# Order of loads, weight preparation and routing at the joints of layer 0 in a four-layer macaron model

## The chip, the cores and the metric

The kernel runs on one core of a Trainium2 chip. A core has a matrix engine (TensorE, PE in the profile; PEld is its weight load), a vector engine (DVE), a scalar engine (ACT) that also evaluates functions from tables, GpSimd (POOL), and SyncE (SP), which here only issues DMA transfers. Each engine works through its own instructions in order and waits on semaphores. SP and ACT each have a DMA queue of their own, so a DMA that ACT issues stands among ACT's other instructions. The metric is the device time of one execution in microseconds (us), lower is better, shown as a median over several runs.

## What is computed

x has 8 sequences of 256 tokens with 128 features, 2048 tokens in all. Four layers follow one another, each a "macaron": half a feed-forward network (FFN), attention or a mixer, and the same FFN again.

```python
x = x + 0.5 * _L0_ffn_ref(_layernorm(x, axis=-1), ...)
x = x + _L0_attn_ref(_layernorm(x, axis=-1), ...)
x = x + 0.5 * _L0_ffn_ref(_layernorm(x, axis=-1), ...)
x = x + 0.5 * _L1_ffn_ref(_layernorm(x, axis=-1), ...)
x = x + _L1_attn_ref(_layernorm(x, axis=-1), ...)
...
```

Layer 0's FFN has 16 experts. Each expert picks its own 256 tokens by the largest scores, and a shared expert treats all tokens. Layer 0's attention has 16 causal heads with rotary positions. Layer 1's FFN has 8 experts of which each token uses two, computed densely with weights that are zero for the others; layer 1's mixer is a selective scan. Layer 2's FFN uses binarized weights, which are computed from `w1` and `w2` alone. The parts that the change touches:

```python
# layer 0 FFN
scores = jax.nn.softmax(flat_x @ gate_w.T, axis=-1).T
topk_weight, topk_idx = jax.lax.top_k(scores, C)        # C = 256 tokens per expert
xg = flat_x[topk_idx]
eo = einsum('eci,edi->ecd', gelu(xg Wg) * (xg Wu), Wd) * topk_weight[..., None]
out = zeros.at[topk_idx].add(eo) + shared
# layer 1 FFN
probs = softmax(xf @ router_w.T) * mask_of_top2
probs = probs / (probs.sum(-1, keepdims=True) + 1e-09)
h = silu(xf gate_w + gate_b) * (xf up_w + up_b)
y = einsum('ne,ned->nd', probs, h down_w + down_b)
# layer 2 FFN, for w1 and w2
alpha = mean(abs(w), axis=1, keepdims=True); bw = alpha * sign(w)
```

## The kernel before

x stays on the core as 16 tiles of 128 tokens by 128 features (`x_res`). Layer 0 treats all 16 tiles at once: FFN (stage 0), attention (stage 1), FFN (stage 2). From layer 1 on the tokens are cut into two halves, a and b, of 4 sequences (class `Half`), whose stages are put into the order listed in `run`: (a,3), then a's scan beside b's first FFN of layer 1, then b's scan beside a's second FFN, and so on. `beside_experts` interleaves the two: the FFN is a generator that yields between its units.

Nobody writes the final order of instructions. A scheduler takes the program's order as priorities and lists the instructions of each engine as their inputs are expected to be ready. An order that must hold can be imposed with a dependency that carries no wait (`add_manual_dep` with class NoSync): it only places an instruction behind another one. DMA transfers of SP and ACT share eight semaphores in turn, so a ninth transfer is issued only when the one before it on its semaphore has landed.

The steps that the change and the prediction touch, with the line numbers of the profile:

- Layer 0's expert weights are 12 transfers of 1 MB (three tensors, four experts in each), issued at L278 at the head of each layer-0 FFN, two of three from SP and one of three from ACT. The norm's bn_stats and bn_aggr (L238, L239) give mean and variance, `rstd` (L226 to L229) the root on ACT, L242 the normalized `xn`, L222 its transposes and L212/L214 their copies to `xnT`. Router: lg (L330), maximum and subtraction (L332, L334), exp (L335), then a bisection for each expert's threshold from L349 on. The shared expert (L431 to L436) runs beside it.
- Expert results are scattered into two accumulators in DRAM; L501 reads them back in eight transfers of 256 KB, from SP and ACT in turn, and L503 adds each into `x_res`. Only four `back` tiles exist.
- Layer 0's attention starts with a norm, then rotations (L727 to L730) and splits into parts (L554 to L557, `sp_r`), which L581 and L582 bring into the layout for scores.
- `l2_weights` (L775 to L794) loads layer 2's `w1` and `w2` (256 KB each) and binarizes and transposes them. It is called after layer 0.
- Layer 1's FFN (`l1_ffn`, L905 on): norm, router lg (L918), maximum L922, exp L925, the choice of two by DVE operations on 128x64 elements (L926 to L951), then the share of the down bias (transposes `prps` L957, products `pb` L963, added at L965), then 8 experts of 2 units of 512 tokens: pg and pu (L976, L978) twice, gs on ACT (L980), hT on DVE (L981), eight po (L987), ys on ACT (L993), x += ys (L995). Expert weights (`w_e`, 384 KB each, three buffers) are loaded at L900, by SP and ACT in turn. The PSUM tiles of pg, pu, lg, prps and the transposes share three buffers; po and pb share a single one.
- Layer 1's scan (`l1_attn`) starts at L1018 and ends with `pout` (L1137).

## Time and profile before

| What | us |
|---|---|
| median of 3 runs (2953.71 to 2966.58) | 2960.93 |
| the profiled execution | 2962.04 |
| its span, first to last instruction | 2960.2 |
| PE busy in the span | 2434.9 (82%) |
| DVE busy | 1592.9 (54%) |
| ACT busy | 1038.1 (35%) |
| POOL busy | 319.2 (11%) |

The mean granted TensorE clock is 0.861 of full speed. The stages that matter here lie at these places of the span: first layer-0 FFN 0 to about 226, attention 226 to 501, second layer-0 FFN 501 to about 728, first layer-1 FFN to 867, then the scans beside the other half's FFN.

In a timeline of the profile each row has the start, the duration, the engine, the line, the operation, output and inputs, shapes and count; in brackets stands how long the engine was idle before and what ended that. "ACTq" and "SPq" are DMA issues by those engines. Rows of windows give busy time (and instruction count) of PE, PEld, DVE, ACT and POOL in a stretch of time, then the granted clock, the DMA engines' busy share and GB/s. All times count from the start of the span.

### The profile page before, as it was taken

What the parts mean: (1) busy time and instruction counts of PE and PEld (TensorE: products, weight loads), DVE (VectorE), ACT (ScalarE), POOL (GpSimd) and SP (SyncE); (2) the same over time, 40 slices, a digit from 0 to 9 for tenths busy, and PEclk for the clock granted to TensorE, in tenths of its full rate; (3) what the DMA queues carried; (4) which work ended last, traced back from release to release, by engine and by line L of the source; (5) the groups of instructions that cost most, each with busy time, mean ns of one, the idle gap of its engine ahead of it and who ended that gap; (6) DMA issues with size and microseconds to landing.
All of it is one profiled execution on the core that took longest, in us unless ns stands there. A gap on an engine that the chain in (4) does not pass through costs nothing.

```text
span 2960.2 us, 40483 instructions
## 1 busy us (share of the span) xinstructions
PE 2434.9 (82%) x16194; PEld 1636.4 (55%) x16194; DVE 1592.9 (54%) x3704; ACT 1038.1 (35%) x1760; POOL 319.2 (11%) x441
## 2 busy tenths in 40 slices
PE   5784888585898889778887699789789789869999
PEld 3572555374554445465456557556556456545666
DVE  6535443834458888658464753554552644453332
ACT  1021333111358576325461332431234422223322
POOL 0371110064000000000000000000300100110000
PEclk9695798688799989867985699899989879979999
DMA  7134333223000000120012000100030100120100
GB/s 247 20 41 110 84 98 146 71 37 78 27 20 26 22 11 16 30 86 23 16 45 75 2 15 22 48 1 23 25 89 5 60 1 15 33 69 22 41 22 22
DMA packets 103018, 136.56 MB, mean 46 GB/s; under 512 B 15161, under 2 KB 84094, under 8 KB 96702
## 3 DMA queue, kind: packets, MB, share of 16 engines
q1 hardware_dynamic: 62858, 84.66, 9.2%
q10 hardware_dynamic: 27684, 39.61, 4.1%
q0 software_dynamic: 12288, 9.71, 2.4%
q8 instruction: 127, 2.08, 0.3%
q14 instruction: 61, 0.50, 0.1%
HBM read 106.27 MB, written 27.53 MB: 45 GB/s over the span
## 4 chain that ended last, share of the span: by engine, by line
PE 50%; DVE 15%; ACT 5%; issue 2%; POOL 1%; DMA 1%; ACTq 0%; DVEq 0%; POOLq 0%; SPq 0%
PE po L1556 7%; PE ph L1544 7%; PE po L987 3%; PE fl L1263 3%; PE pu L978 2%; PE pg L976 2%; PE pbc L1690 2%; PE ctx L649 2%; PE sc L1696 2%; PE y L1710 1%; PE tp L222 1%; DVE h L1116 1%; PE po L1160 1%; DVE hT L981 1%; PE y L1128 1%
## 5 line engine op out<-in xcount | busy, mean ns | idle before, releaser
L1556 PEld LDWEIGHTS po<-w_e,hT 128*128 128x128 f32 x2048 | 259.2, 194 | 71.5 <-issue 45.6
L1556 PE MATMUL po<-w_e,hT 128*128 128x128 f32 x2048 | 277.2, 280 | 10.5 <-DVE hT L1550 8.9
L1544 PE MATMUL ph<-x2T,w_e 128*128 128x512 f32 x512 | 266.5, 626 | 3.2 <-ACT hT L1552 2.8
L1552 ACT ACTIVATE hT<-ph,w_l_cols 128x512 f32<-128x512 f32 x192 | 131.1, 686 | 303.7 <-PE ph L1544 298.1
L602 DVE TENSOR_REDUCE nm<-sc 128x3 f32<-128x384 f32 (+1 forms) x192 | 130.6, 689 | 131.1 <-PE sc L600 130.0
L987 PEld LDWEIGHTS po<-w_e,hT 128*128 128x128 f32 x1024 | 138.3, 202 | 92.5 <-DVE hT L981 52.7
L987 PE MATMUL po<-w_e,hT 128*128 128x128 f32 x1024 | 151.2, 292 | 26.2 <-DVE hT L981 25.5
L639 ACT ACTIVATE pr_e<-scT 128x384 f32<-128x384 f32 (+1 forms) x192 | 111.7, 597 | 168.6 <-PE scT L636 160.7
L222 PE MATMUL tp<-c_ident,xn 128*128 128x128 f32 x208 | 59.0, 405 | 126.9 <-DVE xn L242 112.5
L1562 DVE SCALAR_TENSOR_TENSOR x_res<-po,gt,x_res 128x128 f32<-128x128 f32 x256 | 78.1, 358 | 127.5 <-PE po L1556 127.3
L978 PE MATMUL pu<-xnT,w_e 128*128 128x512 f32 x256 | 135.5, 611 | 10.0 <-ACT gs L980 10.0
L981 DVE SCALAR_TENSOR_TENSOR hT<-pu,w_l_bias,gs 128x512 f32<-128x512 f32 x128 | 95.0, 745 | 86.0 <-PE pu L978 85.3
L976 PE MATMUL pg<-xnT,w_e 128*128 128x512 f32 x256 | 136.8, 616 | 0.0
L481 ACT ACTIVATE gs<-pg 128x512 f32<-128x512 f32 x64 | 38.2, 597 | 252.1 <-PE pg L476 252.1
L980 ACT ACTIVATE gs<-pg,w_l_bias 128x512 f32<-128x512 f32 x128 | 87.7, 689 | 104.8 <-PE pg L976 101.2
L1544 PEld LDWEIGHTS ph<-x2T,w_e 128*128 128x128 f32 x512 | 85.2, 196 | 68.4 <-issue 33.1
L222 PEld LDWEIGHTS tp<-c_ident,xn 128*128 128x128 f32 x208 | 35.3, 177 | 148.6 <-DVE xn L242 72.7
L649 PE MATMUL ctx<-pr_e,vz 128*32 128x256 f32 x512 | 109.2, 402 | 2.8 <-ACT pr_e L639 2.7
L494 POOL DMA_INDIRECT l_acc<-eo,idx x64 | 101.9, 1592 | 34.9 <-DVE eo L493 15.1
L598 PE MATMUL sc<-ks,qs 72*128 72x256 bf16 x256 | 78.2, 306 | 27.5 <-DMA ks<-l_parts 17.5
L1702 DVE TENSOR_TENSOR gw<-sc,dec 128x768 f32<-128x768 f32 x64 | 61.2, 956 | 73.0 <-PE sc L1696 72.8
L993 ACT ACTIVATE ys<-po,pr 128x128 f32<-128x128 f32 x256 | 73.3, 368 | 71.4 <-PE po L987 71.2
(603 smaller groups left out, 5182.1 us busy)
## 6 DMA issues: line engine op xcount, KB each, us to landing
l_parts<-sT SPq DMA_DIRECT2D x48, 192.0 KB, 2.1
qs<-l_parts SPq DMA_DIRECT2D x16, 576.0 KB
w_l_wu<-in_l_wu ACTq DMA_DIRECT2D x8, 1024.0 KB, 8.9
w_l_wg<-in_l_wg SPq DMA_DIRECT2D x8, 1024.0 KB, 14.5
w_l_wd<-in_l_wd SPq DMA_DIRECT2D x8, 1024.0 KB
w_e<-in_l_e SPq DMA_DIRECT2D x16, 512.0 KB, 3.3
w_e<-in_l_e ACTq DMA_DIRECT2D x16, 512.0 KB, 3.6
w_e<-in_l_e ACTq DMA_DIRECT2D x16, 384.0 KB, 4.0
```

The source lines that it names most:

```text
L222: self.nc.tensor.transpose(ps[:, i * P : (i + 1) * P], src_of(g + i), self.ident)
L494: nc.gpsimd.indirect_dma_start(out=accs[h][:, :], out_offset=bass.IndirectOffsetOnAxis(ap=idx[:, j : j + 1], axis=0), in_=eo[:, h, :], in_ ...
L602: nc.vector.tensor_reduce(blocks[:, hp * pr : hp * pr + hp, :], sc[:, :, 0:384].rearrange("p h (k t) -> p h k t", t=P), AX.X, ALU.max, neg ...
L639: nc.scalar.activation(pe, sc[:, :, 0:384], AF.Exp, scale=float(1.0 / np.sqrt(np.float32(8.0))))
L649: nc.tensor.matmul(o, z, pe[:, 0:S], start=(j == 0), stop=False)
L976: self.keep_pace(nc.tensor.matmul(pg, wg[:, c], xnT[:, cols], start=True, stop=True), part)
L978: self.keep_pace(nc.tensor.matmul(pu, wu[:, c], xnT[:, cols], start=True, stop=True), part)
L981: nc.vector.scalar_tensor_tensor(hT[:, k, :], pu, w["l1_bias"][:, 1, e, k : k + 1], gs, ALU.add, ALU.mult)
L987: nc.tensor.matmul(po[:, i, :], hT[:, k, i * P : (i + 1) * P], wd[:, k * P : (k + 1) * P], start=(k == 0), stop=(k == 1),)
L1544: mm = nc.tensor.matmul(ps, we[:, k * P : (k + 1) * P], xnew[:, 512 * g : 512 * g + 512], start=True, stop=True)
L1552: nc.scalar.activation(hT[:, k, :], ps, AF.Relu, bias=bias)
L1556: nc.tensor.matmul(po[:, i, :], hT[:, k, i * P : (i + 1) * P], we[:, (4 + k) * P : (5 + k) * P], start=(k == 0), stop=(k == 3),)
```

## The change

Five things are changed; no operation is added or removed.

1. The loads of layer 0's experts become a function of their own. In the first FFN all 12 are issued by ACT and are ordered behind the root of the norm; the second FFN issues them as before.
2. Layer 1's expert loads are ordered behind the last read-backs of the same queue (`backs`).
3. `l2_weights` is called between the attention and the second layer-0 FFN. Its temporary tiles lie on the other side of the memory, and its PSUM pool has one buffer instead of two.
4. Where a scan runs beside the other half's FFN, that FFN's first bn_stats is ordered behind the first half's finished routing, and its first transpose behind the first half's fourth unit of experts (`hold`, `held`).
5. In layer 1's FFN the part of the down bias becomes `biases()`, called ahead of the third expert, with its transposes ordered behind the pg of the unit before.

```diff
         self.flip = 0
+        self.backs = [None, None]
...
         pass
+
+    def held(self, inst, queue):
+        pass
+
+    def behind(self, inst, mark):
+
+        dep = mybir.DependencyInfo(mybir.DependencyClass.NoSync, mybir.DependencyReason.DATA)
+        self.tc.add_manual_dep(inst.ins, mark.ins.name, dep, reason="what is needed first goes first")
...
             for i in range(m):
-                self.nc.tensor.transpose(ps[:, i * P : (i + 1) * P], src_of(g + i), self.ident)
+                self.held(self.nc.tensor.transpose(ps[:, i * P : (i + 1) * P], src_of(g + i), self.ident), "tensor")
             self.evict(dst[:, g * P : (g + m) * P], ps[:, : m * P])
...
         self.nc.vector.tensor_scalar(s, var, eps, None, ALU.add)
-        self.nc.scalar.activation(s, s, AF.Sqrt)
+        self.root = self.nc.scalar.activation(s, s, AF.Sqrt)
         self.nc.vector.reciprocal(s, s)
...
         for t in range(NT):
-            nc.vector.bn_stats(st[:, t, :], self.x[:, t, :])
+            self.held(nc.vector.bn_stats(st[:, t, :], self.x[:, t, :]), "vector")
             nc.vector.bn_aggr(mv[:, t, :], st[:, t, :])
...
             w[n] = pool.tile(list(src.shape), F32, name=f"w_{n}", tag=f"w_{n}")
+        return w
+
+    def l0_experts_in(self, w, after=None):
+
         for e in range(0, 16, 4):
-            for i, n in enumerate(w):
-                (self.nc.sync, self.nc.scalar)[i % 2].dma_start(w[n][:, e : e + 4], self.ins[n][:, e : e + 4])
-        return w
+            for i, n in enumerate(("l0_wg", "l0_wu", "l0_wd")):
+                eng = self.nc.scalar if after else (self.nc.sync, self.nc.scalar)[i % 2]
+                dma = eng.dma_start(w[n][:, e : e + 4], self.ins[n][:, e : e + 4])
+                if after:
+                    self.behind(dma, after)
...
-    def l0_ffn(self, w):
+    def l0_ffn(self, w, first):
         nc, tc = self.nc, self.tc
...
             w = w | self.l0_experts(ctx.enter_context(tc.tile_pool(name="l0x", bufs=1, side="right", reuse_waits="tile")))
+            if not first:
+                self.l0_experts_in(w)
             pool = ctx.enter_context(tc.tile_pool(name="l0f", bufs=1, reuse_waits="tile"))
...
                 xn, xnT = self.norm(rp, psA, width=W)
+                if first:
+                    self.l0_experts_in(w, self.root)
                 lg = ps1.tile([P, NT, 16], F32, name="lg", tag="pre")
...
                         back = ep.tile([P, 4, D], F32, name="back", tag="back", bufs=4)
-                        (nc.sync, nc.scalar)[k].dma_start(back, accv[k][:, 4 * g : 4 * g + 4, :])
+                        self.backs[k] = (nc.sync, nc.scalar)[k].dma_start(back, accv[k][:, 4 * g : 4 * g + 4, :])
                         xs = self.x[:, 4 * g : 4 * g + 4, :].rearrange("p t d -> p (t d)")
...
         with ExitStack() as ctx:
-            tmp = ctx.enter_context(tc.tile_pool(name="l2b", bufs=1, reuse_waits="tile"))
-            psum = ctx.enter_context(tc.tile_pool(name="l2bps", bufs=2, space=PSUM, reuse_waits="tile"))
+            tmp = ctx.enter_context(tc.tile_pool(name="l2b", bufs=1, side="right", reuse_waits="tile"))
+            psum = ctx.enter_context(tc.tile_pool(name="l2bps", bufs=1, space=PSUM, reuse_waits="tile"))
             w1, w2 = self.load(tmp, "l2_w1"), self.load(tmp, "l2_w2")
...
         tc = self.tc
-        with tc.tile_pool(name="l0w", bufs=1, side="right", reuse_waits="tile") as wp:
-            w0 = self.l0_weights(wp) if (on(0) or on(1) or on(2)) else None
-            if on(0):
-                self.l0_ffn(w0)
-            if on(1):
-                self.l0_attn(wp)
-            if on(2):
-                self.l0_ffn(w0)
-
-
-
         with tc.tile_pool(name="l2w", bufs=1, reuse_waits="tile") as late:
-            w2 = self.l2_weights(late) if (on(6) or on(8)) else None
+            with tc.tile_pool(name="l0w", bufs=1, side="right", reuse_waits="tile") as wp:
+                w0 = self.l0_weights(wp) if (on(0) or on(1) or on(2)) else None
+                if on(0):
+                    self.l0_ffn(w0, True)
+                if on(1):
+                    self.l0_attn(wp)
+
+                w2 = self.l2_weights(late) if (on(6) or on(8)) else None
+                if on(2):
+                    self.l0_ffn(w0, False)
+
+
+
             a, b = (Half(self, k, w2) for k in range(2))
...
         self.steps, self.pace, self.marks = [], [], None
+        self.backs, self.units, self.hold = chip.backs, [], {}
...
+    def held(self, inst, queue):
+
+        mark = self.hold.pop(queue, None)
+        if mark is not None:
+            self.behind(inst, mark)
+
     def beside_experts(self, other):
...
         other.pace, other.marks = self.steps, self.SCAN_MARKS
+        if self.units:
+            other.hold = {"vector": self.routed, "tensor": self.units[3]}
         fill = other.l1_ffn()
...
             t = pool.tile([P, src.shape[2]], F32, name="w_e", tag="w_e", bufs=3)
-            (self.nc.sync, self.nc.scalar)[e % 2].dma_start(t, src[e])
+            dma = (self.nc.sync, self.nc.scalar)[e % 2].dma_start(t, src[e])
+            if self.backs[e % 2] is not None:
+                self.behind(dma, self.backs[e % 2])
             yield e, t
...
             nc.vector.tensor_scalar(sm, sm, 0.5, None, ALU.mult)
-            nc.vector.tensor_tensor(pr, pr, wide(sm), ALU.mult)
-            prT = pool.tile([E, T], F32, name="prT", tag="prT")
-            G = T // 512
-            for g in range(G):
-                ps = psum.tile([E, 512], F32, name="prps", tag="h")
-                for i in range(4):
-                    nc.tensor.transpose(ps[:, i * P : (i + 1) * P], pr[:, 4 * g + i, :], self.ident)
-                self.evict(prT[:, 512 * g : 512 * g + 512], ps)
-            for g in range(G):
-                po = pso.tile([P, 4, D], F32, name="pb", tag="o")
-                for i in range(4):
-                    t = 4 * g + i
-                    nc.tensor.matmul(po[:, i, :], prT[:, t * P : (t + 1) * P], w["l1_bd"], start=True, stop=True)
-                xs = self.x[:, 4 * g : 4 * g + 4, :]
-                nc.vector.tensor_tensor(xs, xs, po, ALU.add)
+            self.routed = nc.vector.tensor_tensor(pr, pr, wide(sm), ALU.mult)
+
+            def biases():
+                prT = pool.tile([E, T], F32, name="prT", tag="prT")
+                for g in range(G):
+                    ps = psum.tile([E, 512], F32, name="prps", tag="h")
+                    for i in range(4):
+                        tr = nc.tensor.transpose(ps[:, i * P : (i + 1) * P], pr[:, 4 * g + i, :], self.ident)
+                        self.behind(tr, self.units[-1])
+                    self.evict(prT[:, 512 * g : 512 * g + 512], ps)
+                for g in range(G):
+                    po = pso.tile([P, 4, D], F32, name="pb", tag="o")
+                    for i in range(4):
+                        t = 4 * g + i
+                        nc.tensor.matmul(po[:, i, :], prT[:, t * P : (t + 1) * P], w["l1_bd"], start=True, stop=True)
+                    xs = self.x[:, 4 * g : 4 * g + 4, :]
+                    nc.vector.tensor_tensor(xs, xs, po, ALU.add)
+
+            G, self.units = T // 512, []
             for e, we in self.experts(pool, "l1_e"):
...
                     part = (G * e + g) / (8 * G)
+                    if (e, g) == (2, 0):
+                        biases()
                     yield part
...
                         pg = psum.tile([P, 512], F32, name="pg", tag="h")
-                        self.keep_pace(nc.tensor.matmul(pg, wg[:, c], xnT[:, cols], start=True, stop=True), part)
+                        mm = nc.tensor.matmul(pg, wg[:, c], xnT[:, cols], start=True, stop=True)
+                        self.keep_pace(mm, part)
                         pu = psum.tile([P, 512], F32, name="pu", tag="h")
...
                         )
+                    self.units += [mm]
                     po = pso.tile([P, 4, D], F32, name="po", tag="o")
```

## Prediction

> **What bounds the kernel now.** I read the windows of 50 us first, to find stretches in which no engine is full, then the timelines of the engines inside those stretches. All times are us from the start of the span. The change touches four joints of the first 800 us, so these windows matter (columns: PE, PE weight load, DVE, ACT, POOL busy, TensorE clock, DMA share, GB/s):
>
> ```profile
> 0.00:50.00 50.00, 29.41 (x109) 19.42 (x110) 24.58 (x109) 11.10 (x15) 1.86 (x9) 1.00 0.95 338
> 700.00:750.00 50.00, 15.65 (x76) 12.52 (x75) 24.72 (x79) 7.83 (x11) 6.57 (x5) 0.61 0.40 103
> 750.00:800.00 50.00, 40.63 (x156) 26.36 (x156) 23.06 (x73) 13.59 (x27) 0.00 (x0) 0.68 0.04 13
> 800.00:850.00 50.00, 50.00 (x233) 31.06 (x233) 19.08 (x28) 23.39 (x56) 0.00 (x0) 1.00 0.10 32
> 900.00:950.00 50.00, 46.16 (x180) 26.68 (x181) 45.22 (x47) 42.88 (x59) 0.21 (x1) 0.95 0.05 16
> ```
>
> From 800 on PE is the bound: work taken off the way there shortens the kernel one for one. Between 700 and 783 nothing is full: a chain of small steps hops between engines, and PE runs at 0.5 to 0.7 of its clock. From 900 to 1020 DVE, ACT and PE are all near 90%: work that lands there costs time. At the start ACT is held by its own DMA issues, and in the middle (ACT's timeline) it is ready long before it is needed:
>
> ```profile
> 0.74 15.52 ACTq L278 DMA_DIRECT2D w_l_wu<-in_l_wu  x4
> 16.29 1.28 ACT L228 ACT_TABLE_LOAD   x1 [16.29 <-DMA w_l_sd<-in_l_sd]
> 17.58 0.22 ACT L228 ACTIVATE ln_s<-ln_s 128x16 f32<-128x16 f32 x1
> ...
> 33.68 0.42 ACT L335 ACTIVATE sc<-sc 128x256 f32<-128x256 f32 x1 [0.54 <-DVE sc L334]
> ```
>
> ```profile
> 493.30 1.90 ACTq L278 DMA_DIRECT2D w_l_wu<-in_l_wu  x4
> 495.31 1.28 ACT L228 ACT_TABLE_LOAD   x1 [1.43 <-issue]
> 506.19 0.21 ACT L228 ACTIVATE ln_s<-ln_s 128x16 f32<-128x16 f32 x1 [9.59 <-DVE ln_s L227]
> ```
>
> PE's timeline at the joint into layer 1 shows what stands ahead of the first expert: two norms and routings in turn, both halves' bias parts (prps, pb), then pg. Once running, a unit of two pg, two pu and eight po comes every 788.83 - 783.50 = 5.33.
>
> ```profile
> 753.75 2.18 PE L222 MATMUL tp<-c_ident,xn 128*128 128x128 f32 x8 [5.75 <-DVE xn L242]
> 756.10 3.56 PE L918 MATMUL lg<-w_l_router,xnT 128*128 128x8 f32 x16 [0.17 <-issue]
> 760.10 1.87 PE L957 MATMUL prps<-c_ident,pr 128*8 128x128 f32 x8 [0.45 <-DVE pr L951]
> ...
> 771.01 1.87 PE L957 MATMUL prps<-c_ident,pr 128*8 128x128 f32 x8 [4.13 <-DVE pr L951]
> ...
> 774.81 2.08 PE L976 MATMUL pg<-xnT,w_e 128*128 128x512 f32 x2
> ...
> 783.50 1.02 PE L976 MATMUL pg<-xnT,w_e 128*128 128x512 f32 x2
> ...
> 788.83 1.02 PE L976 MATMUL pg<-xnT,w_e 128*128 128x512 f32 x2
> ```
>
> **Joint 0, the start: -5.** DVE's first bn_stats waits for x until 9.43 and its sum of steps up to ln_s ends at 13.95, but the sqrt comes at 17.58, since ACT issues expert loads until 16.26 and then loads a table (1.28). After, all 12 expert loads are queued on ACT behind the sqrt. The sqrt then follows x: at 14.0 if x still lands at 9.43, at about 8.4 if x, without the wu loads beside it, lands between 3.7 and 8. From xn to the router's maximum took 32.76 - 18.41 = 14.35. That puts the maximum at about 25, plus one shared-expert step that PE now does earlier. Against it stand 12 issues on ACT ahead of the exp. An issue that need not wait takes 0.33 to 0.48, but the row above has four that took 15.5 together, because at most eight transfers are outstanding; the twelfth waits for the fourth to land. Four MB at the window's 338 GB/s is 12.4, so the queue is free at about 24 to 26 and the exp runs near 28.5 where it ran at 33.68. Bounds: -9 if only x sets it; +5 if the loads on one queue go at half that rate (24.8, exp near 38.5). I take -5. The weights land by about 48 and the first expert needs them near 100, behind a DVE chain: hidden by 50. The four zero stores and the table store on SP only gain by the eight loads taken from that queue.
>
> **Joint 1, into the attention: +3.** Layer 2's weights are now made here. The 256 KB of w1 go ahead of the first read-back while scatters are still awaited (DVE idle 6.60 before 226.17): hidden. The 256 KB of w2 go between two read-backs: the read-backs with 768 KB of expert loads among them took 712.50 to 727.83 = 15.3, without them 223.26 to 236.39 = 13.1, so 256 KB cost 2.2/3 = 0.7. Seven DVE operations (0.16, 0.42, 4 x 0.68 and 0.42, by rows of like shape: 0.61 to 0.70 for 128x512) come in one block of 3.2 between the rotations (end 248.84) and sp_r (249.89, 1.06 of idle): 3.2 - 1.06 = 2.1. Those in other gaps, one Abs on ACT (0.61) and a reduce of 0.69 in the gap of 1.29 before 247.16, are covered. Sum 2.8. PE is 85% busy for the next 200 us, so a late start passes through. Bounds 0.5 (block behind the queries' wait) to 5 (w2 ahead of a read-back whole).
>
> **Joint 2, into the second FFN: +6.** DVE gets 0.60 + 0.60 + 0.08 + 0.34 + 4 x 0.60 = 4.0 of w2T among the bn_stats, which run without a gap from 501.63 to 505.98, so ln_s is ready at about 510. ACT now does w2T's copy (behind PE's transposes, some 509.1 to 509.7), then the four wu issues (1.90) and the table load (1.28) that it did at 493 to 497 before: sqrt at 512.9, where it was 506.19. These issues wait for no transfer of their own set, since the first eight outstanding places hold all four. Low 3.8 (DVE alone), high 9 (issues spread as 0.6 each); I take 6. The 12 MB start at about 508 instead of 491; 251 GB/s in that window moves them by 558, the first expert needs them after 600: hidden by 40.
>
> **Joint 3, into layer 1: -28.** Removed from the chain: expert loads among the read-backs (2.2, above); w1T's operations between the xn (731.86 to 737.8; 0.62 + 0.33 + 3 x 0.60 + 0.34 + 0.61 = 3.7). So xnT moves from 740.15 to about 734.5. PE's order has pg, pu right behind four to eight lg, so the first pg stands at 736 to 737 instead of 774.81: 38. What stood ahead does not vanish. Inside the stream now come: lg (3.6 cold), this half's prps and pb (1.87 + 4.1 cold, half of that at full clock: 3), the other half's tp and lg (5.7 cold, 2.9). The first ys waits for the routing: from the maximum at 741, a table load (1.28), exp (0.42), 23 DVE operations of 0.24 = 5.6 with two hT (0.75) among them and four ys (1.1) give 751. The tile po has one buffer, so until then PE can do the first unit and pg, pu of two more: 5.33 + 2 x 3.44 = 12.2, from 736.5 to 748.7: 3 more. Three further table loads on ACT (3 x 1.28), which is 2.9 of 5.33 busy by four ys (0.37) and two gs (0.69), fit in its gaps. Against that, the first unit took 783.50 - 774.81 = 8.7 with pb inside it, 3 over. 38 - 3.6 - 3 - 2.9 - 3 + 3 = 28.5. The half's own expert weights are issued on SP behind all read-backs, at about 724 to 726, and land 3.3 to 4.0 later, ahead of xnT. Bounds: -32 (routing covered: 28.5 + 3) to -15 (every insertion at its cold price, 3.6 + 6 + 5.7, plus four table loads, 5.1, and a routing stall of 5.6).
>
> [...]
>
> **Later stages: 0.** The other half's routing (5.6), its x += pb and its prT copies (2 x 0.69 + 0.7) now land at the start of the scan stage, where DVE idles 4 + 6 between 860 and 900 but all is full after: +5. In return the next two first-layer FFNs start ahead of their bias parts, where PE idled 10 in 1020 to 1040 and 8.24 before 1264.68: -3 and -2. Ten table loads fewer are off the way mostly. Bounds -8 to +15.
>
> **Sum.** -5 + 3 + 6 - 28 + 0 = -24 against the profiled execution, 2962.04 (span 2960.2), which stands 1.1 above the median 2960.93. So 2938 by the profile, 2937 by the median; I say 2938.
>
> **Rivals.**
> 1. Joint 3 gives half: routing and table changes hold the stream and the scan stage pays +10. -5 + 3 + 6 - 15 + 10 = -1: 2960. For it: DVE and ACT at 43 to 45 of 50 from 900 on. Against: 40 us of nearly empty PE ahead of it.
> 2. Slower: the scan stages take the routing badly. The same chain inside a scan's set-up ran 17 instead of 5.6:
>
> ```profile
> 1045.39 0.23 DVE L922 TENSOR_REDUCE mx<-lg 128x8 f32<-128x64 f32 x1 [2.92 <-PE lg L918]
> ...
> 1061.93 0.17 DVE L947 TENSOR_SCALAR sm<-sm 128x8 f32<-128x8 f32 x1
> ```
>
> PE is in order; if pg and po stand ahead of the scan's products and wait for that chain, each of two stages loses 17 and 5.1 of table loads: +44. -24 + 44 = +20: 2981. It decides from a stage loss of 39 on. Against: the first expert there started at 882 only, so its ys needs the chain late.
> 3. Joint 0 doesn't do what it says: ACT full of issues, +5 instead of -5: 2948.
> 4. The l2 weights cost their upper bounds (5 and 9): 2943, inside the likeliest case.
>
> **Chances.** Likeliest (2925 to 2948) 0.58; rivals 1 and 3 together 0.24; rival 2 0.13; better still, near 2920, 0.05. A measurement here tells 0.5% (14.8) from no change: faster is below 2946.1, slower above 2975.7. Of the likeliest case a tenth lies above 2946: 0.58 x 0.9 + 0.05 = 0.57, and 0.03 of rivals 1 and 3 below it make faster 0.6; of rival 2 nearly all, and 0.02 of unforeseen losses, make slower 0.15; same 0.25. Range: from 2920 (-9 + 3 + 3.8 - 32 - 8 = -42) to 2964 (rival 1 with the spread of the runs, some 4, above it).
>
> **What would show it.** Right: sqrt below 12 and exp below 30 at the start; sp_r some 3 later than x's last add allows now; the second norm's sqrt 5 to 7 later after the attention's last add; the first pg within 15 of the last read-back's add; first-half FFN's last add about 24 earlier than 866.93. Wrong: pg there in time but its units 8 and more apart; the scan stage (first scan step to pout) longer by over 10; exp at the start later than 33.68.

## The result, and the profile after

The change makes the kernel faster: the median goes from 2959.15 us (four runs, 2953.71 to 2966.58) to 2927.77 us (four runs, 2927.05 to 2930.21). The ratio is 0.9894, with a 95% interval from 0.9871 to 0.9917: some 31 us, or 1.1%. The profiled execution has a span of 2925.3 us where it was 2960.2, 35.0 less; the granted clock is 0.865 where it was 0.861.

The clearest way to see where the time went is to read the same events in both timelines and to watch how the difference grows.

| Event | before | after | after - before | this stretch gave |
|---|---|---|---|---|
| root of the first norm (ACT) | 17.58 | 8.78 | -8.80 | |
| first step of the bisection (DVE) | 39.65 | 32.89 | -6.76 | |
| last result of an expert, first FFN | 219.31 | 212.53 | -6.78 | joint 0: -6.8 |
| first `sp_r` of the attention | 249.89 | 247.08 | -2.81 | joint 1: +4.0 |
| last x += of the attention | 501.71 | 494.12 | -7.59 | attention: -4.8 |
| root of the second FFN's norm | 506.19 | 504.68 | -1.51 | joint 2: +6.1 |
| last result of an expert, second FFN | 707.90 | 704.49 | -3.41 | experts: -1.9 |
| first pg of layer 1 | 774.81 | 731.95 | -42.86 | |
| last x += ys of the first half | 867.63 | 831.00 | -36.63 | joint 3: -33.2 |
| last x += pout of the first scan | 1032.87 | 999.66 | -33.21 | first scan: +3.4 |
| last x += ys of layer 1 | 1485.11 | 1452.51 | -32.60 | +0.6 |
| end | 2960.25 | 2925.27 | -34.98 | -2.4 |

The last stretch and the attention from `sp_r` on run the same operations in both kernels, and so do the experts of the second FFN. Over all the profiles of this study the attention took between 244.6 and 251.8 from `sp_r` to its last x +=, the experts between 199.8 and 203.1 (but for e8, with 214.7), and the last stretch between 1472.6 and 1483.0. So single profiles differ by up to 7, 3 and 10 us there, and the -4.8, -1.9 and -2.4 are no effect of the change that can be told from this spread. The granted clock of the stretch goes with it: in the attention it was 0.81 before and 0.83 after.

The windows of the kernel after, at the places shown of before (columns as there: PE, PE weight load, DVE, ACT, POOL busy with counts, clock, DMA share, GB/s):

```profile
0.00:50.00 50.00, 30.15 (x130) 19.55 (x131) 30.11 (x137) 10.89 (x16) 1.81 (x9) 0.93 0.95 341
700.00:750.00 50.00, 25.48 (x100) 17.01 (x99) 23.77 (x87) 12.83 (x20) 5.59 (x4) 0.66 0.36 96
750.00:800.00 50.00, 49.54 (x223) 30.17 (x222) 21.73 (x38) 23.12 (x55) 0.00 (x0) 0.97 0.13 40
800.00:850.00 50.00, 41.27 (x178) 23.94 (x177) 30.32 (x88) 20.87 (x46) 0.40 (x5) 0.86 0.02 6
900.00:950.00 50.00, 46.65 (x186) 26.05 (x185) 44.40 (x46) 39.98 (x58) 0.00 (x0) 1.00 0.10 30
```

PE is full from 750 to 800, at 0.97 of its clock, where before it was busy for 40.63 of 50 at 0.68; the set-up of the scan, where it isn't, now begins at 831 and so falls into the window from 800. The scan's window, 900 to 950, looks as it did. At the start the DMA engines move 341 GB/s, where it was 338, but ACT's timeline shows another order:

```profile
0.74 1.28 ACT L237 ACT_TABLE_LOAD   x1 [0.74 <-PEq L1870]
8.78 0.21 ACT L237 ACTIVATE ln_s<-ln_s 128x16 f32<-128x16 f32 x1 [6.76 <-DVE ln_s L236]
...
18.97 0.34 ACTq L292 DMA_DIRECT2D w_l_wd<-in_l_wd  x1
20.72 0.58 ACT L223 COPY xnT<-tp 128x512 f32<-128x512 f32 x1 [6.96 <-PE tp L231]
...
27.84 0.33 ACTq L292 DMA_DIRECT2D w_l_wd<-in_l_wd  x1
28.21 1.28 ACT L354 ACT_TABLE_LOAD   x1 [6.90 <-DMA w_l_wg<-in_l_wg]
29.50 0.42 ACT L354 ACTIVATE sc<-sc 128x256 f32<-128x256 f32 x1
```

The root now waits for DVE alone, no longer for ACT's own issues. But ACT's queue stands still twice. In the trace the transfers of SP and ACT use eight semaphores in turn (101 to 108): ACT's third issue starts at 18.97, 0.02 behind the last landing of the transfer before it on its semaphore (18.95), and the twelfth at 27.84, 0.02 behind that of the fourth (27.82). The first wait costs nothing that can be seen: the copy of `xnT` behind it starts at 20.72, when PE has just finished the transposes that it copies. The second has the exp behind it. The router's maximum runs at 25.30 and the subtraction behind it ends at 26.18, so the exp at 29.50 comes 3.3 later than it could: in this profile that is the price of 12 issues on this queue.

It is not paid in every profile. In the seven other kernels below that have the same 12 issues on ACT, the exp (28.6 to 30.2) follows the subtraction by 0.2 or less; there the maximum itself comes later, at 27.6 to 29.3. The cause shows in PE's rows: in the kernel after, a pair of matmuls of 128x512 takes 1.02 to 1.10 from 22.50 on, in the others the pair at 23 to 24 still takes 2.05 and the next one 1.66 to 1.92 (as in e14, shown below). So the start of the bisection is much the same, 32.0 to 33.6, with two different steps coming last.

At joint 1, DVE's timeline after shows layer 2's operations (L807 to L813) as one block ahead of `sp_r`:

```profile
242.82 0.28 DVE L749 TENSOR_TENSOR rt<-qkv,c_cos 128x128 f32<-128x128 f32 x1
243.02 0.17 DVE L807 TENSOR_SCALAR w1Tal<-w1Tal 128x4 f32<-128x4 f32 x1
...
243.55 0.82 DVE L810 TENSOR_TENSOR w1T<-w1T,w1T 128x512 f32<-128x512 f32 x1
...
247.08 0.75 DVE L574 TENSOR_TENSOR sp_r<-qk,sp 128x256 f32<-128x256 f32 x2
```

The block lasts from 243.02 to 247.08. At joint 2, ACT's timeline after has the copy of `w2T`, the four issues and the table load between the attention's last x += (494.12) and the root:

```profile
501.39 0.59 ACT L223 COPY w2T<-tp 128x512 f32<-128x512 f32 x1 [6.21 <-PE tp L231]
501.39 1.90 ACTq L292 DMA_DIRECT2D w_l_wu<-in_l_wu  x4
503.38 1.28 ACT L237 ACT_TABLE_LOAD   x1 [1.41 <-issue]
504.68 0.22 ACT L237 ACTIVATE ln_s<-ln_s 128x16 f32<-128x16 f32 x1
```

At joint 3, PE's timeline after shows one norm's transposes, half of the router's products, and then at once the first pg:

```profile
727.83 2.27 PE L231 MATMUL tp<-c_ident,xn 128*128 128x128 f32 x8 [23.99 <-DVE xn L251]
730.22 1.88 PE L949 MATMUL lg<-w_l_router,xnT 128*128 128x8 f32 x8
731.95 2.05 PE L1013 MATMUL pg<-xnT,w_e 128*128 128x512 f32 x2
...
741.05 1.17 PE L1013 MATMUL pg<-xnT,w_e 128*128 128x512 f32 x2
...
747.92 1.95 PE L1026 MATMUL po<-w_e,hT 128*128 128x128 f32 x16
...
757.56 0.82 PE L989 MATMUL prps<-c_ident,pr 128*8 128x128 f32 x6
```

The pg pair takes 2.05 at first and is near its full rate (1.17; 1.02 from 744.48 on) nine us later; the granted clock is 0.50 from 731.95 to 741.05 and 0.98 in the nine us behind that. The part of the bias (`prps`) now stands inside the stream of experts. ACT's first ys, which frees the tile po, waits for the routing until 746.56:

```profile
746.56 1.14 ACT L1032 ACTIVATE ys<-po,pr 128x128 f32<-128x128 f32 x4 [0.33 <-DVE pr L982]
```

### The profile page after: what moved, and what is told of

Same layout as the page of the kernel before. It is cut to its first block, busy times and chain, and to the rows that moved or that the text cites. A ratio compares the mean times of both kernels' runs of the same rounds, so it can differ in the third digit from the quotient of the medians.

```text
span 2925.3 us, 40469 instructions
## 1 busy us (share of the span) xinstructions
PE 2419.1 (83%) x16194; PEld 1625.1 (56%) x16194; DVE 1590.1 (54%) x3704; ACT 1022.0 (35%) x1750; POOL 320.3 (11%) x441
## 4 chain that ended last, share of the span: by engine, by line
PE 50%; DVE 15%; ACT 5%; DMA 2%; issue 2%; POOL 2%; ACTq 0%; DVEq 0%; POOLq 0%; SPq 0%
PE po L1595 7%; PE ph L1583 7%; PE po L1026 3%; PE pu L1016 3%; PE fl L1302 3%; PE pg L1013 2%; PE pbc L1729 2%; PE ctx L668 2%; PE sc L1735 2%; PE y L1749 1%; PE tp L231 1%; DVE h L1155 1%; PE po L1199 1%; PE y L1167 1%; PE po L1652 1%
## 5 line engine op out<-in xcount | busy, mean ns | idle before, releaser
L617 PE MATMUL sc<-ks,qs 72*128 72x256 bf16 x256 | 77.2, 302 | 31.4 <-DMA ks<-l_parts 20.3
```

## The experiments

The questions were three. Which of the five parts gives what? Joint 3 gave 33.2, so does that come from the order that parts 4 and 5 impose, or from taking layer 2's weights out of the joint (part 3)? And can the prices at joints 0, 1 and 2 be avoided? Every ratio is to the kernel before, on the same chip in the same session.

The intervals below are read from the timelines, as in the table above: "start" to the first bisection step; "joint 1" from the first FFN's last expert result to `sp_r`; "attn" from `sp_r` to the attention's last x +=; "joint 2" from there to the root; "experts" from there to the second FFN's last expert result; "backs" from there to the last read-back's x +=; "pg" from there to the first pg; "half" from the last expert result to the first half's last x += ys (it contains "backs" and "pg").

| Kernel | ratio (95%) | start | joint 1 | attn | joint 2 | experts | backs | pg | half | end |
|---|---|---|---|---|---|---|---|---|---|---|
| before | 1 | 39.65 | 30.58 | 251.82 | 4.48 | 201.71 | 19.93 | 46.98 | 159.73 | 2960.25 |
| after | 0.9894 (0.9871, 0.9917) | 32.89 | 34.55 | 247.04 | 10.56 | 199.81 | 18.96 | 8.50 | 126.51 | 2925.27 |
| e2_start_old | 0.9916 (0.9900, 0.9933) | 39.14 | 34.55 | 248.80 | 10.56 | 202.07 | 17.75 | 8.50 | 122.33 | 2930.85 |
| e5_no_backs | one run | 32.92 | 34.71 | 244.58 | 10.61 | 201.45 | 17.36 | 8.50 | 122.86 | 2928.86 |
| e3_no_hold | 0.9901 (0.9884, 0.9917) | 33.00 | 34.39 | 244.79 | 10.54 | 201.56 | 19.46 | 9.23 | 127.65 | 2925.96 |
| e4_bias_first | 0.9947 (0.9930, 0.9963) | 32.02 | 33.78 | 246.79 | 10.58 | 201.15 | 19.12 | 20.59 | 130.39 | 2933.92 |
| e6_joint3_undone | 0.9944 (0.9924, 0.9964) | 33.22 | 33.17 | 247.62 | 10.59 | 200.57 | 19.79 | 23.52 | 135.52 | 2940.49 |
| e1_l2_late | 0.9917 (0.9900, 0.9933) | 31.99 | 30.81 | 247.35 | 4.47 | 201.86 | 20.53 | 21.03 | 138.90 | 2937.21 |
| e7_only_l2 | 0.9953 (0.9936, 0.9969) | 38.72 | 34.55 | 250.39 | 10.62 | 200.20 | 16.79 | 23.52 | 137.36 | 2943.65 |
| e12_temp_right | 0.9915 (0.9897, 0.9933) | 38.65 | 30.00 | 248.17 | 4.47 | 202.62 | 16.14 | 26.68 | 136.05 | 2937.17 |
| e8_l2_in_experts | 0.9893 (0.9875, 0.9911) | 32.52 | 30.15 | 248.34 | 4.48 | 214.74 | 19.44 | 8.51 | 123.95 | 2930.81 |
| e9_start_two_queues | 0.9886 (0.9863, 0.9908) | 29.46 | 34.52 | 250.30 | 10.57 | 199.96 | 19.07 | 8.50 | 126.65 | 2928.34 |
| e13_l2_spread | 0.9874 (0.9853, 0.9895) | 33.56 | 30.43 | 251.60 | 4.48 | 200.65 | 19.30 | 8.50 | 124.35 | 2923.38 |
| e14_spread_two_queues | 0.9854 (0.9832, 0.9876) | 32.76 | 30.72 | 248.23 | 4.47 | 203.11 | 18.46 | 8.50 | 124.18 | 2915.24 |

The half too differs without a cause in the program: it took 122.3 to 126.7 in the seven kernels that have the same joint 3 as the kernel after (after, e2, e5, e8, e9, e13, e14; e5 lacks part 2 only). The two longest, after and e9, had a granted clock of 0.94 from the first pg to the half's end, the other five 0.95 to 0.97. So joint 3 is worth 33 to 37 us against the one profile of before, and a difference of under 4 there is not one that can be told from the spread.

### The parts undone one at a time

**Part 1 undone** (from the kernel after):

```diff
-            if not first:
-                self.l0_experts_in(w)
+            self.l0_experts_in(w)
...
-                if first:
-                    self.l0_experts_in(w, self.root)
```

> The changed kernel with the first FFN's expert loads issued at its head by SP and ACT as before (part 1 undone). Theory: the first bisection operation, 32.9 in the changed kernel, is back at 39.6 and all later marks move by the same 6.8: ratio 0.9894 + 0.0023 = 0.9917. Rival (the start is hidden behind something later, such as the expert loads' landing or the gathers): the bisection is back at 39.6 but the last eo of the first FFN stays at 212 to 214, ratio 0.9894.

The median was 2933.23. The bisection starts at 39.14, 6.25 later than in the kernel after, and the last expert result keeps 6.0 of that. So joint 0 is worth 6 to 7 us, and nothing downstream hides it.

**Part 2 undone:**

```diff
-            if self.backs[e % 2] is not None:
-                self.behind(dma, self.backs[e % 2])
```

> The changed kernel with layer 1's expert loads not ordered behind the read-backs (part 2 undone). Theory A (the 2.2 us that the read-backs of the second FFN took longer than the first's came from the expert loads among them): from the last eo to the last read-back's add 20.5 to 22 instead of 18.96. Theory B (that stretch differs from run to run by as much: 16.8 with the loads among them when only layer 2's weights were moved, 17.8 to 20.5 behind the ordering): anywhere between 16.5 and 20.5, the whole time within 8 us of the changed kernel's.

There is one run of this kernel, 2930.65. The read-backs take 17.36, against 18.96 with the order, and the first pg stands 8.50 behind them in both. Over all kernels the read-backs take between 16.1 and 20.5, with no relation to this part: the lowest value belongs to e12, a kernel without it, and one near the highest, 19.93, to the kernel before, without it as well. The order of part 2 gives nothing that can be seen here, as theory B expected.

**Part 4 undone:**

```diff
-        if self.units:
-            other.hold = {"vector": self.routed, "tensor": self.units[3]}
```

> The changed kernel without the ordering of the other half's norm behind the first half's routing (part 4 undone), the bias part still ahead of the third expert. Theory (moving the bias part is what brings the first experts forward; the order of the program alone puts the first half first): the first pg stands 8 to 11 behind the last read-back's add (8.5 in the changed kernel), the other half's transposes and router products go among the first two units, and the first half's last ys add is within +4 us of the changed kernel's; ratio 0.9894 to 0.991. Rival (the ordering is what does it): first pg 20 or more behind the last read-back's add, the half's end 10 later, ratio 0.993 or more.

The median was 2929.13, 1.4 above that of the kernel after in another session, within the runs' spread. The first pg comes 0.7 later and the half ends 1.1 later, which is less than the spread of the half. Alone the hold is worth about one us at most: the first pg at 9.23 shows that the first half goes ahead without it.

**Part 5 undone:**

```diff
-                        self.behind(tr, self.units[-1])
...
+            biases()
             for e, we in self.experts(pool, "l1_e"):
...
-                    if (e, g) == (2, 0):
-                        biases()
```

> The changed kernel with the bias part ahead of the first expert again (part 5 undone), the other half's norm still held. Theory: the first pg has to wait for router products (3.6), table load and exp (1.5), 23 routing operations (5.6), prps, prT and pb (about 6): 24 to 28 behind the last read-back's add instead of 8.5, the half's end 12 to 16 later (3 of the bias part and some of the thin start fall away), and the later stages that start with their routing lose 3 more: ratio 0.9894 + 0.005 to 0.0065 = 0.994 to 0.996. Rival (PE was going to wait for the routing anyway, at the first ys): the half's end less than 5 later, ratio below 0.991.

The median was 2941.74. The ratio is the theory's, but its reason is not: the first pg comes 12.1 later (20.59 against 8.50), and the half ends only 3.9 later, where the theory had 12 to 16 and the rival under 5. Most of the lead of an early pg is lost again while the routing runs, so an early pg is no measure of the gain. In the profile 4.5 more are lost in the scans, where the FFN beside each has its bias part first again: 1.5 up to the end of the first scan (its last x += pout) and 3.0 from there to the end of the second. The profiled run, 2935.74, is the fastest of the four; the rest of the 14 us between the medians isn't located.

**Parts 4 and 5 undone together:**

```diff
-        if self.units:
-            other.hold = {"vector": self.routed, "tensor": self.units[3]}
...
-                        self.behind(tr, self.units[-1])
...
+            biases()
...
-                    if (e, g) == (2, 0):
-                        biases()
```

> The changed kernel with parts 4 and 5 undone together: bias part ahead of the experts and the other half's norm not held. Undone alone, the first cost the half's end 3.9 us (from the last eo of the second FFN: 126.5 to 130.4) and the second 1.1. Theory A (they cover for each other: with both undone the two norms and routings stand in a row on DVE and PE again): first pg 25 to 32 behind the last read-back's add, the half's end 140 to 146 behind the last eo, ratio 0.995 to 0.998. Theory B (the two add up): first pg about 21, the half's end 131 to 132 behind eo, ratio 0.993 to 0.995.

The half takes 135.52, 9.0 more than in the kernel after, where the two alone cost 1.1 and 3.9. That lies between the two forecasts (140 to 146 if they cover for each other, 131 to 132 if they add up), nearer to adding up: 4 us over the sum is the size of the spread. The more important number is that 135.52 is still 24 below the kernel before. In these profiles the orders of parts 4 and 5 make 9 of the 33 us; 24 come without them.

**Part 3 undone:**

```diff
-            tmp = ctx.enter_context(tc.tile_pool(name="l2b", bufs=1, side="right", reuse_waits="tile"))
-            psum = ctx.enter_context(tc.tile_pool(name="l2bps", bufs=1, space=PSUM, reuse_waits="tile"))
+            tmp = ctx.enter_context(tc.tile_pool(name="l2b", bufs=1, reuse_waits="tile"))
+            psum = ctx.enter_context(tc.tile_pool(name="l2bps", bufs=2, space=PSUM, reuse_waits="tile"))
...
-                w2 = self.l2_weights(late) if (on(6) or on(8)) else None
...
+            w2 = self.l2_weights(late) if (on(6) or on(8)) else None
```

> The changed kernel with layer 2's weights made after layer 0 again (part 3 undone). Theory (the attention and the second FFN take the two delays back, so part 3 costs and brings little): from the last eo of the first FFN sp_r starts 30.6 later as before the change (34.6 with it), yet the attention's last add stays 281 to 283 behind that eo; the second FFN's sqrt comes 4.5 behind that add instead of 10.6; w1T and w2T come back between the read-backs and the first pg, which goes from 8.5 to 15 to 19 behind the last read-back's add. Sum against the changed kernel: -4 (sqrt, with 2 of 6 recovered) + 8 = +2 to +5 us, ratio to the kernel before 0.990 to 0.991. Rival (a later start of the attention passes through, and its shorter time was something else): the last ao add is 277 to 278 behind eo, and the whole is 0 to -4 against the changed kernel, 0.988 to 0.9895.

The median was 2936.81. Joints 1 and 2 fall back to what they were (30.81 and 4.47), and the half takes 138.90. PE's timeline of this kernel shows why:

```profile
722.79 1.12 PE L231 MATMUL tp<-c_ident,w1T 128*128 128x128 f32 x4 [27.50 <-DVE w1T L813]
728.87 1.09 PE L231 MATMUL tp<-c_ident,w2T 128*128 128x128 f32 x4 [4.96 <-DVE w2T L813]
733.46 2.18 PE L231 MATMUL tp<-c_ident,xn 128*128 128x128 f32 x8 [3.50 <-DVE xn L251]
```

Both transposes of layer 2's weights stand ahead of the first norm's, so DVE makes both weights before it gets to the norm. Part 3 is thus worth 12.4 at joint 3 in the presence of the others (138.90, against 122.3 to 126.7 in the kernels that have it), against 3.7 and 6.1 paid at joints 1 and 2. How much of the 3.7 survives the attention is not clear from one pair, since its length varies by itself. Over all profiles the stretch from the first FFN's last expert result to the attention's last x += has a mean of 281.8 in the eight kernels with these operations in it (279.2 to 284.9) and 279.7 in the six without (278.2 to 282.4): about 2 of the 4, with overlapping ranges.

### What in part 3 gives the time

**Part 3 alone, on the kernel before:**

```diff
-            tmp = ctx.enter_context(tc.tile_pool(name="l2b", bufs=1, reuse_waits="tile"))
-            psum = ctx.enter_context(tc.tile_pool(name="l2bps", bufs=2, space=PSUM, reuse_waits="tile"))
+            tmp = ctx.enter_context(tc.tile_pool(name="l2b", bufs=1, side="right", reuse_waits="tile"))
+            psum = ctx.enter_context(tc.tile_pool(name="l2bps", bufs=1, space=PSUM, reuse_waits="tile"))
...
+                w2 = self.l2_weights(late) if (on(6) or on(8)) else None
...
-            w2 = self.l2_weights(late) if (on(6) or on(8)) else None
```

> The kernel before with nothing but layer 2's weights moved (part 3 alone). Theory A (its price at joints 1 and 2 is paid in full, its gain at joint 3 is the 12.4 that undoing it cost there in the changed kernel): sp_r +3.7, second sqrt +6.1 behind the attention's last add, the half's end 159.7 - 12 = 147 to 149 behind the last eo, sum -2 to -4 us: ratio 0.9985 to 1.000. Theory B (at the kernel before only w1T's 3.7 and half of w2T's operations were in the chain; the rest ran beside the first half's routing): the half's end 152 to 156 behind the last eo, ratio 1.000 to 1.0025.

The half takes 137.36: 22.4 less than before, more than either forecast allowed. So parts 1, 2, 4 and 5 without part 3 (e1) give 20.8 there, part 3 alone gives 22.4, and all together 33.2. The two are substitutes for a good part; they do not add up.

The 3.7 us of w1T's operations that stood among the `xn` are too few for 22.4. The timelines of the kernel before hold two more hints. On SP's queue, layer 2's `w1` and `w2` are loaded behind the read-backs, and the router's weights are loaded twice, for the two halves, the second time late:

```profile
707.28 0.35 SPq L205 DMA_DIRECT2D w_l_router<-in_l_router  x1
...
722.10 0.81 SPq L205 DMA_DIRECT2D w_l_w<-in_l_w  x2
...
737.06 0.33 SPq L205 DMA_DIRECT2D w_l_router<-in_l_router  x1
```

And on DVE the norm that comes second starts only when PE has finished with `w2T`:

```profile
748.04 0.49 DVE L238 BATCH_NORM_STATS2 bnst<-x_res 128x6 f32<-128x128 f32 x2 [0.35 <-PE tp L222]
```

The temporary tiles of layer 2's weights lie on the left side of the memory, where the tiles of the first half's FFN are to go as well; those of the other half lie on the right. So by this reading the first half, whose experts PE waits for, cannot load its router's weights or start its norm until the temporary tiles are free, and the scheduler lets the other half go first. (The names in the profile do not tell the halves apart; the order of PE before fits this, as the first pg stands behind the bias transposes of both halves.) The test changes one word of the kernel before and leaves the call where it is:

```diff
-            tmp = ctx.enter_context(tc.tile_pool(name="l2b", bufs=1, reuse_waits="tile"))
+            tmp = ctx.enter_context(tc.tile_pool(name="l2b", bufs=1, side="right", reuse_waits="tile"))
```

> The kernel before, its only edit being that the temporary pool of layer 2's weights lies on the right side of the memory instead of the left; the weights are still made after layer 0. Theory A (what moving the weights brought at joint 3, 22 us, is not the DVE operations alone: on the left the temporary tiles take the place that the first half's tiles need, so the other half's norm and routing went first; on the right the first half goes first): the first half's norm is the first one, the first pg 33 to 38 behind the last read-back's add instead of 47, the half's end 148 to 152 behind the last eo instead of 159.7, ratio 0.996 to 0.998. Theory B (it was the operations and their transposes in the chain): 156 to 161 behind the last eo, ratio 0.9985 to 1.0015.

The median was 2938.88, beside 2961.91 of the kernel before in the same session: 23 us for one word, and more than was expected of it (pg 26.68, half 136.05). PE's timeline of this kernel:

```profile
707.97 1.11 PE L222 MATMUL tp<-c_ident,w2T 128*128 128x128 f32 x4 [4.96 <-DVE w2T L794]
724.91 2.17 PE L222 MATMUL tp<-c_ident,xn 128*128 128x128 f32 x8 [15.82 <-DVE xn L242]
727.25 3.56 PE L918 MATMUL lg<-w_l_router,xnT 128*128 128x8 f32 x16 [0.17 <-issue]
730.66 2.61 PE L222 MATMUL tp<-c_ident,xn 128*128 128x128 f32 x8
...
746.04 2.08 PE L976 MATMUL pg<-xnT,w_e 128*128 128x512 f32 x2
```

The transposes of `w2T` are done at 709, while the read-backs are still awaited, where the kernel before did them at 746.89 to 748.00. Both norms then follow each other at once, and none of layer 2's operations stands among them. The first pg now stands behind the bias transposes of one half only (742.24; the other's come at 834.01). The reason is not only the free place on the left, as SP's queue of this kernel shows:

```profile
593.13 0.82 SPq L205 DMA_DIRECT2D w_l_w<-in_l_w  x2
```

The loads come 129 us earlier in the span than before (722.10), and DVE makes `w1T` from 597.29 to 607.4, beside the second FFN's first expert. The call stands where it stood, but with a place that is free sooner the scheduler moved the work itself out of the joint. So one word gives as much at joint 3 as part 3 alone (136.05 and 137.36), without the 4 and 6 us at joints 1 and 2: e12 is 6 below e7 by the medians of two sessions. How much of the 23 comes from the work being gone from the joint, and how much from the left side being free for the first half, no run separates, since e12 and e7 change both; theory A named only the second.

### Without the prices

**Layer 2's weights at one place inside the second FFN's experts** (from the kernel after, with the same place for the temporary tiles):

```diff
+                    if e == 4 and not first:
+                        self.w2 = self.l2_weights(self.late, ps, scaled)
...
-                nc.scalar.activation(a, src, AF.Abs)
+                self.behind(nc.scalar.activation(a, src, AF.Abs), mark)
...
-                nc.vector.tensor_scalar(b, src, 0.0, None, ALU.is_lt)
+                self.behind(nc.vector.tensor_scalar(b, src, 0.0, None, ALU.is_lt), mark)
```

> The changed kernel with layer 2's weights loaded and made at the fifth expert of the second layer-0 FFN, ordered behind the expert before, their transposes in that stage's PSUM tiles. Theory (a late start of the attention and of the second norm passes through; DVE is busy 16 of 50 in the expert stage): sp_r 30.8 behind the last eo (34.6 in the changed kernel), second sqrt 4.5 behind the attention's last add (10.6), the expert stage 0 to 3 longer by a block of 8 DVE operations, joint 3 unchanged: -7 to -10 us, ratio 0.986 to 0.987. Rival (the attention or the second FFN takes the delays back, as its shorter time in the profile of the changed kernel suggested): -1 to -4, ratio 0.988 to 0.989.

The median was 2928.71. Joints 1 and 2 are free of the work (30.15 and 4.48), but the experts take 214.74, some 13 more. PE's timeline of this kernel at that place:

```profile
619.70 1.60 PE L507 MATMUL po<-w_l_wd,hT 128*128 128x128 f32 x12 [0.41 <-DVE hT L503]
626.73 1.12 PE L231 MATMUL tp<-c_ident,w1T 128*128 128x128 f32 x4 [5.42 <-DVE w1T L814]
632.80 1.09 PE L231 MATMUL tp<-c_ident,w2T 128*128 128x128 f32 x4 [4.95 <-DVE w2T L814]
```

PE takes its instructions in order, so it stood idle for 5.42 and 4.95 until DVE had made what the transposes need, and the next expert stood behind them. That is 10.4 of the 13. Neither forecast had this: the time stayed at that of the kernel after (2927.77), where -7 to -10 was expected.

**The same work spread over the experts:** `l2_weights` becomes a generator that does two operations per expert from the second on; its transposes come three steps of the generator behind the last of them (in the trace 4.0 behind the end of w1T's last operation), and its temporary tiles lie in the pool of the finished weights.

```diff
+                    if work is not None and e >= 1:
+                        self.late_mark = scaled
+                        for _ in range(2):
+                            next(work, None)
...
+                self.behind(op(), self.late_mark)
+                yield
+            yield
+            yield
...
+            self.hold_tr = self.late_mark
             self.transpose_tiles(w[name], lambda k: flat[:, k * P : (k + 1) * P], 4, psum)
```

> The changed kernel with layer 2's weights made during the experts of the second layer-0 FFN as in the run with one block, but two operations behind each expert, and the transposes two experts behind their last operation. Theory (the block's 13 us came from PE, in order, waiting at the transposes for a chain of eight DVE operations): sp_r 30.2 to 30.8 behind the last eo, second sqrt 4.5 behind the attention's last add, from that sqrt to the last eo 200 to 203 (214.7 with the block, 199.8 to 202.1 without), joint 3 as in the changed kernel: -7 to -10 us against it, ratio 0.986 to 0.987. Rival (the added DVE operations themselves hold the expert stage, which runs scatter and gather on GpSimd at 40 of 50): 207 or more, ratio 0.9885 or more.

The median was 2924.69. The experts take 200.65, as in kernels without this work, joints 1 and 2 are free, and the first pg keeps its place. PE's row of the first transposes has no wait for DVE in it:

```profile
641.81 0.60 PE L233 MATMUL tp<-c_ident,w1T 128*128 128x128 f32 x4
```

So the 13 us were the waiting in one place, and the work itself has room beside the experts; whether the spreading or the later transposes did it is not separated. In the total e13 is 3.1 below the kernel after, by medians of two sessions and with overlapping intervals, where -7 to -10 was forecast: the attention, the same program, took 251.60 in its profile.

**The start's loads on two queues** (from the kernel after):

```diff
-                eng = self.nc.scalar if after else (self.nc.sync, self.nc.scalar)[i % 2]
+                eng = (self.nc.sync, self.nc.scalar)[i % 2]
```

> The changed kernel with the first FFN's expert loads from SP (two of three) and ACT (one of three), those of ACT still behind the norm's root. Theory (12 issues on ACT hold the copies of xnT and the exp: in the changed kernel the second copy waited for an issue until 20.7 and the exp until 28.2): sqrt at 8.3 to 9, router maximum at 19 to 23, first bisection operation at 27 to 30 instead of 32.9, -3 to -6 us, ratio 0.9875 to 0.9885. Rival (SP's loads, issued while x is still on the way, take x's bandwidth, as the four wu loads did before the change): sqrt at 11 to 15, bisection at 33 to 36, ratio 0.989 to 0.9905.

The median was 2927.99 (2917.97 to 2930.16). The bisection starts at 29.46, 3.4 earlier than in the kernel after, with the router's maximum at 25.30 in both: the wait of the exp behind ACT's twelfth issue is gone, and the exp follows the subtraction at once:

```profile
25.30 0.42 DVE L351 TENSOR_REDUCE mx<-lg 128x16 f32<-128x256 f32 x1 [8.35 <-PE lg L349]
26.22 0.42 ACT L354 ACTIVATE sc<-sc 128x256 f32<-128x256 f32 x1 [3.14 <-DVE sc L353]
```

The last expert result is 3.3 earlier too. The copy of `xnT`, which the theory had waiting for an issue until 20.7, starts at 20.53: it had waited for PE in both. In the total nothing is to be seen (attention 250.30 in this profile, against 247.04). And the 3.4 hold only where PE is at its full rate by 22.50, as it is in these two profiles and in no other kernel with part 1: in the others the maximum comes after ACT's issues anyway.

**Both:** the edits of the last two kernels together.

> The run before with the first FFN's expert loads from SP and ACT in turn as well. Theory: the two edits are at different joints and add up: bisection at 29.5, the last eo of the first FFN at 208.5 to 209.5, -10 to -13 us against the changed kernel, ratio 0.985 to 0.986. Rival (loads of the two queues meet the attention's or the later stages' transfers): bisection at 29.5, ratio 0.987 or more.

This is the fastest kernel of the study: 2916.80 (2914.93 to 2925.46), a ratio of 0.9854 (0.9832 to 0.9876), 45 us below the kernel before in the same session and 8 below e13. The ratio is the theory's, but its start is not: the bisection begins at 32.76, not near 29.5, as the router's maximum came at 28.45, and the last expert result is just 1.0 ahead of e13's. PE's rows ahead of that maximum show why:

```profile
23.13 2.06 PE L454 MATMUL pu<-xnT,w_l_su 128*128 128x512 f32 x2
24.97 1.91 PE L452 MATMUL pg<-xnT,w_l_sg 128*128 128x512 f32 x2
```

The same pairs took 1.10 (22.50) and 1.02 (23.44) in the kernel after. Of the 8 us by which the two profiles differ in span, 6.8 lie in the last stretch (1472.63 against 1479.47, at a granted clock of 0.89 against 0.88), whose program is the same in both. Over whole runs it is alike: three of e14's four had a mean clock of 0.872 and 2914.93 to 2917.03 us, the fourth 0.866 and 2925.46; e13's had 0.866 to 0.869. Whether the program brought the higher clock is not shown, so of e14's lead only about 1 us can be put down to the two queues.

## Why the prediction was right

The forecast was "faster", 2938 us; 2927.77 is 10 below it and inside the range. Each step against its measurement:

- **Joint 0, -5: measured -6.8.** The root came at 8.78, near the 8.4 for an x that lands early, the maximum at 25.30 (forecast about 25) and the exp at 29.50 (28.5). ACT's wait for the twelfth transfer was read rightly from the row with four issues in 15.5, but that it came last is luck of this profile: in seven other kernels with the same issues PE's slower matmuls held the maximum to 27.6 to 29.3, and the exp came as late by that way. Taking part 1 back cost 6.3 (e2).
- **Joint 1, +3: measured +4.0.** The block stands where it was foreseen, but takes 4.1 instead of 3.2: two of its 128x512 operations took 0.82 and 0.83, not 0.68, and one of `w2T` (0.67) joined it. "A late start passes through" is half shown: about 2 of the 4 are left at the attention's end, in means whose ranges overlap.
- **Joint 2, +6: measured +6.1**, by the steps named: copy, issues, table load, root.
- **Joint 3, -28: measured -33.2.** The lead of pg was put at 38 and is 39.5: 1.0 in the read-backs and 38.5 behind them. What is paid back inside the stream was put at 9.5 and measured 6.2 (99.05 from the first pg to the half's last x += ys, where it was 92.82). The first ys came at 746.56, 14.6 behind the first pg, as the forecast had it (736.5 to 751, 14.5). Yet PE shows no idle time from 731.95 to 749.70, where 3 us of stall were put: its work until then, the first unit and pg and pu of two more, was put at 12.2 and took 16.0 (731.95 to 747.92), as the first unit ran at a granted clock of 0.50 with half of the router's products inside it.
- **Later stages, 0: measured +3.4 up to the end of the first scan and +0.6 from there to the end of layer 1.** The +5 came as +3.4. The -3 and -2 of earlier first experts in the other FFNs do not show in this sum, though undoing part 5 cost 3.0 there (e4).

The sum of the terms that the change touches is -6.8 + 4.0 + 6.1 - 33.2 + 3.4 + 0.6 = -25.9, beside the predicted -24. The other 9 us of the profile's 35.0 lie in stretches whose operations did not change. The medians differ by 31.4, so 5 to 6 us of the gain are not the forecast's mechanism, and the sum of -25.9 comes as near to -24 as it does partly because its terms missed in opposite ways (-1.8, +1.0, +0.1, -5.2 and +4.0).

What the prediction had wrong is the share of the causes at joint 3. It credited layer 2's weights there with 3.7 for operations among the `xn`, and "expert loads among the read-backs" with 2.2. The runs show 22.4 for part 3 alone, 12.4 for it in the presence of the others, 23.7 for the place of its tiles alone (which moved the work as well), and nothing for the read-backs. The 38 came out because it was counted from the place of pg, after all parts, and not as a sum over parts.

The rivals: joint 3 at half its gain needed +10 in the scan stage, which had +3.4; the slower case needed a stage loss of 39, against the same +3.4, and windows 900 to 950 look alike; the start at +5 did not come. A table load took its 1.28 here and no further time beside it: after the loads at 28.21 (1.28) and 503.38 (1.28) the next ACTIVATE starts 0.01 and 0.02 behind the load's end, and the load at 29.93 starts 0.01 behind the end of the ACTIVATE ahead of it (29.50, 0.42). PE was idle for 23.99 up to 727.83, and the first pairs of pg and pu behind that took 2.05, 2.06, 1.91 and 1.91. The stream was at 1.17 a pair by 741.05, so the pg and pu of one unit ran at about half their later rate, at a granted clock of 0.50.

## What to carry to other kernels

Look at where temporary tiles lie before moving work: here one word, the side of the memory of a short-lived pool, let the scheduler do the work 129 us earlier without moving the call, and was worth 23 us. Then look in the timeline at where the work went, since an edit that seems to move nothing can move it. Work taken off a joint was free beside a stream of matmuls when it was spread out, with each PE operation behind the operations that feed it (the experts took 200.65 and 203.11 in e13 and e14, 199.8 to 202.1 in the kernels without this work); as one block the same work cost 13 us there. Undo parts singly and together before crediting them: two causes that each give 21 to 22 us alone gave 33 together.

## What was not expected of the hardware

The same program does not take the same time at the same place: the attention ran between 244.6 and 251.8 us in these profiles. The granted TensorE clock goes with it: the two shortest attentions (244.58 and 244.79) had 0.85 and 0.86 over that stretch, the two longest (251.82 and 251.60) 0.81 and 0.83. Which of the two is the cause is not shown, as PE was also granted 0.50 behind a wait of 23.99 (from 731.95 to 741.05 above). A gain of 3 us in one stage, like e9's, can be read at its own marks but not from one total, and even there only as far as the same step comes last.

## What stays open

Three things were not tried or not settled. The orders of parts 1, 4 and 5 with the call of layer 2's weights where the kernel before has it, but their temporary tiles on the right side, were not run. No run has the weights made early with the first half's place still taken, or late with it free, so the two causes inside part 3 stay unseparated. And why PE reached its full rate by 22.50 in two profiles and later in the others is not shown, nor is whether e14's higher clock comes from its program.
